# Three edits to the set-up order of a four-layer kernel: transposes of second image halves, the second square root, the next lines

## The chip, the cores and the metric

The kernel runs on one core of a Trainium2 chip. The metric is device time in microseconds of one execution; the figure used is the median of several. A core has five engines with a queue each, worked off in order: TensorE (PE; its weight loads are shown as PEld), VectorE (DVE), ScalarE (ACT), GpSimd (POOL) and SyncE (SP), which here issues most of the DMAs. TensorE writes to banks of PSUM; a bank can be written again only when an engine has copied it out. The operands of all other work lie in SBUF, 128 partitions wide.

## The reference, cut to what matters

The input is 1024 images of 16 x 16 pixels with 16 channels. Four layers follow each other, each of the form x + f(group norm of x):

```python
def _gn(v, G=8, eps=1e-5):
    B_, H_, W_, C_ = v.shape
    g = v.reshape(B_, H_, W_, G, C_ // G)
    m = jnp.mean(g, axis=(1, 2, 4), keepdims=True)
    s = jnp.var(g, axis=(1, 2, 4), keepdims=True)
    return ((g - m) / jnp.sqrt(s + eps)).reshape(v.shape)
...
x = x + _L0_conv_ref(_gn(x), core0, core1, core2)     # tensor train, 4096 x 4096
x = x + _L1_conv_ref(_gn(x), ...)                     # cellular automaton step
x = x + _L2_conv_ref(_gn(x), filters, bias)           # 3 x 3 convolution
x = x + _L3_conv_ref(_gn(x), ...)                     # cellular automaton step
```

Only the start of the first layer matters here. There an image is a vector of 16 x 16 x 16 values, and the layer multiplies it by a 4096 x 4096 matrix given by three small cores. Ahead of that the images have to be normalised: per image and per group of two channels, minus the mean, times one over the root of the variance.

## The kernel before, in words

**Order.** Every engine works off its instructions in exactly the order in which the program emits them (manual schedule); waits between engines are put in where data or a buffer demands them. So the place of a call in the program is its place in the queue of each engine that it uses, SP's DMA queue among them. `now(steps)` emits steps at once. `run(main, us, loads, *spans)` emits the steps of a phase one after the other, and weaves background steps in between: a span `(steps, lo, hi)` spreads its steps, by their weights, from the fraction `lo` to the fraction `hi` of the phase's main steps.

**Layer 0.** The 1024 images are worked in two chunks of 512; chunk 0 is the first to be set up. The matrix product is done by a Strassen-like scheme: 13 phases (`NP`, list `OUTER`), each with four units of seven products (`INNER`), each product two main steps of four matmuls of a 128 x 256 block, in the profile `po` L1693. Phase 0 has 56 main steps. Its order is made by hand: steps 0 to 7 are the products 0 and 2 of units 0 and 1, then follow the rest of unit 0 (steps 8 to 17), of unit 1 (18 to 27), and units 2 and 3. The weights of a unit's products are built on TensorE from 32 small matmuls into four banks (`build`, L1579), copied out by ScalarE (L1584) and combined by VectorE (`mix`, L1608 and L1610). The products are gathered from their banks by ScalarE (L1737) and VectorE (L1731, L1741), and at the end of a unit `store` writes them to memory (L1666).

**Set-up of chunk 0** (`first_images`). The images of chunk 0 arrive as eight pieces of 1024 KB: `load(half, bg)`, with four groups of 128 images (`bg`) and two halves of the 16 image rows. Groups 0 and 1 (i = 0) are fetched first, groups 2 and 3 (i = 1) later; the pieces lie in the tile of pair 1 (`XN[1]`) until that pair's lines come in.
- `stats` and `aggregate` (VectorE, L1116 and L1149) make mean and variance per image and group.
- `turn` fills one bank with four 128 x 128 transposes on TensorE (L1123), and ScalarE copies the bank out. For the first half of the rows the copy goes into a raw block of tile 0 (L1126), `raw_block(wh, i)`; for the second half it goes into a line tile (L1130), and every second bank the line tile is stored to the scratch tensor `xr` in memory by SP (`kept`, L1136, 512 KB). `turns(half, i, wh)` is four such banks. The banks rotate over two tags, one with a single buffer, one with four.
- `keep(wh, i)` stores a whole raw block to `xr` too (L1136, 1024 KB).
- `root(i)` adds epsilon on VectorE (L1153) and takes the square root on ScalarE (L1154); `newton(i)` refines the reciprocal on VectorE (L1158 to L1162); `widen(k, i)` spreads mean (k = 0) or reciprocal root (k = 1) over the row (L1169); `spread(k, i)` turns that with two transposes (L1177) and a copy on ScalarE (L1178).
- `first_normed(b, i)`, called x00, x10, x01 and x11, takes the mean away and scales, two steps each on VectorE (L1280). Block x11 is written over its own raw block; the sums of blocks (`combined`, L1309) are written over the others.

**Around it.** `early` builds a part of the core's weights and, after the second group of loads, stores them to `g_dram` (`keep_g`, L652 and L659, twelve DMAs on SP). `rest` is twelve further pieces of these weights, woven into phase 0 at fixed steps: TensorE (L645), a copy on ScalarE to one small buffer (L697), and after every second piece again six stores on SP (L652, L659); the next piece's copy has to wait for them, since the buffer is the same. `gload` fetches weights for a coming unit (L1546, 256 KB). `part_steps(1)` prepares the lines of pair 1 for phase 1: three loads of 1024 KB from `xr` by SP (L1338), a pause, eight steps of centring and scaling, the fourth load, eight more (all L1280), saves to memory (L1344), then additions (L1348, L1421, L1431): 32 steps of equal weight on VectorE in all.

The dictionary `before` at L2214 says which pieces of set-up are emitted ahead of which main step of phase 0.

Of the kernel before, what the change touches and what calls it, by code (L numbers as in the profile page):

```python
# [105 lines left out]
def conv_preact_kernel(ctx: ExitStack, tc: tile.TileContext, a: dict, out: bass.AP):  # L106
# [1175 lines left out]
    def first_normed(b, i):  # L1282

        X, E = part_tile(0)
        cols = slice(256 * i, 256 * i + 256)

        def op(t, k):
            x = X[:, b, t : t + 4, i]
            centre_scale(x, raw_block(b, i)[:, t : t + 4], 0, cols, k)

        return [(1.2, lambda t=t, k=k: op(t, k)) for t in (0, 4) for k in range(2)]
# [826 lines left out]
    def run(layer, us, loads, *spans, by=0.0):  # L2118

        start, main = layer
        start()
        loads, done = list(loads), 0
        todo = []
        for bg, lo, hi in spans:
            bg = [b if isinstance(b, tuple) else (1, b) if callable(b) else (b, None) for b in bg]
            idle = sum(b[0] for b in bg if b[1] is None) / (us * (hi - lo))
            less = min(1.0, 0.7 / idle) if idle else 1.0  # L2130
            weight = sum(b[0] for b in bg if b[1] is not None) or 1.0
            at = lo
            for cost, step in bg:
                if step is None:
                    at += cost * less / us
                else:
                    todo.append((at, step))
                    at += (hi - lo) * (1 - idle * less) * cost / weight
        todo.sort(key=lambda x: x[0])
        for i, step in enumerate(main):  # L2140
            step()
            part = (i + 1) / len(main)
            while done < len(loads) and done < len(loads) * part / (by or 1e-9):
                loads[done]()
                done += 1
            while todo and (todo[0][0] < part or i == len(main) - 1):
                near = getattr(step, "dense", True) or i == len(main) - 1
                if getattr(todo[0][1], "beside", False) and not near:
                    break
                todo.pop(0)[1]()  # L2150
# [7 lines left out]
    def steps_of(*more):  # L2158
        return (lambda: None), [x for m in more for x in m]

    def now(steps):
        for step in steps:
            step = step[1] if isinstance(step, tuple) else step
            if callable(step):
                step()
# [5 lines left out]
    with ExitStack() as es:  # L2171
# [3 lines left out]
        load, stats, turns, keep, aggregate, root, newton, widen, spread = first_images(tag)  # L2175
        for bg in range(2):
# [12 lines left out]
        stats(1, 1)  # L2189
        aggregate(0)  # L2190
        aggregate(1)
        now(turns(0, 0, 0))
        root(0)
        widen(0, 0)
        newton(0)
# [8 lines left out]
        x00, x11, x10, x01 = (first_normed(*at) for at in ((0, 0), (1, 1), (1, 0), (0, 1)))  # L2204
# [3 lines left out]
        now(x10[0::2] + x10[1::2])  # L2208
        mix(1, "s2")
        now(more[0:2])  # L2210
        half1 = [turns(1, i, 0) + turns(1, i, 1) for i in range(2)]
        late0, late1 = turns(0, 1, 0), turns(0, 1, 1)
        rest = rest[0] + rest[1]
        before = {  # L2214
# [2 lines left out]
            + late1[:2],  # L2217
            5: [lambda: keep(1, 0), lambda: keep(0, 0)],
            6: late1[2:] + [lambda: keep(1, 1)] + late0[:2],
            8: late0[2:] + [lambda: build(1, 0), lambda: keep(0, 1)] + half1[0][:4]  # L2220
            + [lambda: root(1), lambda: widen(0, 1), lambda: newton(1)]
            + half1[0][4:] + [lambda: spread(0, 1), lambda: widen(1, 1)]
            + half1[1][:2] + [lambda: spread(1, 1)]
            + x11[0::2] + x11[1::2] + half1[1][2:4],
            9: [catch_up] + more[2:6],
            10: rest[:1],
            11: rest[1:2] + x01[0::2] + x01[1::2],
# [13 lines left out]
        def sums_late(j):  # L2241
            c = combined(j)
            woven_into(j, {2 * k + 1: c[2 * k : 2 * k + 2] for k in range(5)})
# [2 lines left out]
        woven_into(0, before)  # L2246
        for j in late:
            sums_late(j)
        run(steps_of(phases[0]), 107, (), (part_steps(1), 0.3, 0.99))
        loads, stat, lines, tail, more = input_steps(["m", "w"], G)  # L2250
        tail += [(0, more[0]), 2, (0, more[1]), 2]
        stat = [[stat[0][i] for i in range(4)], [(2.6, s1[1]) for s1 in stat[1][0::2]], stat[1][1::2]]
# [8 lines left out]
        root = {}  # L2261
# [89 lines left out]
```

## Time and profile before

| | us |
|---|---|
| median of 3 runs | 2723.96 (2723.88 to 2724.68) |
| the profiled execution, its own time | 2722.89 |
| its span, from the first to the last instruction | 2720.6 |
| TensorE, 0 to 10 us | busy 3.60 |
| 10 to 20 us | busy 6.37 |
| 20 to 30 us | busy 7.43 |
| 50 to 60 us | busy 7.90 |
| 60 to 70 us | busy 8.11 |
| 100 to 130 us | busy 30.00 |

How to read the lines that follow further down. A line of the timeline gives the start of a group of like instructions, how long the group took, the engine (PE, PEld, DVE, ACT, POOL; SPq is SyncE issuing DMAs), the line of the program, the operation, what it writes and reads, how many there were, and in brackets how long the engine had been idle before it and what released it. A line of the table by stretches gives a stretch in us from the start, its length, the busy time of PE, PEld, DVE, ACT and POOL with the number of instructions, the granted clock of TensorE as a share of full speed, the busy share of the DMA engines, and GB/s moved.

### The profile page before, as it was taken

The page shows a single profiled execution, that of the slowest core. Times are in us where ns is not written, and L with a number is a line of the kernel's source. Part 1 is how long each engine was busy: PE and PEld are TensorE (multiplying, and loading weights), DVE is VectorE, ACT ScalarE, POOL GpSimd, SP SyncE. Part 2 cuts the span into 40 slices and gives each one's busy share as a digit, 9 for nine tenths or more (in the row PEclk, how much of TensorE's full clock was granted, in tenths as well). Part 3 has the DMA queues.
Part 4 walks back from the last instruction along what each step waited for, and adds up shares of the span by engine and source line. Part 5 has one row for each costly group of instructions (what it writes and reads, how often), then busy time and mean ns, then how long its engine had stood idle before and what let it go on. Part 6 is the DMA issues. An engine that isn't in the chain of part 4 may idle for free.

```text
span 2720.6 us, 47297 instructions
## 1 busy us (share of the span) xinstructions
PE 2662.2 (98%) x18990; PEld 1744.2 (64%) x18990; DVE 1994.4 (73%) x2422; ACT 1241.3 (46%) x2094; POOL 539.2 (20%) x701
## 2 busy tenths in 40 slices
PE   7999999999999999999999999999999999999997
PEld 6888888888888888888778633333333333334344
DVE  8796768867787777577878677658778858856654
ACT  5224222222232222333322376776767757666664
POOL 1011352221132633212322111111113211110000
PEclk9999999999999999999999999999999999999998
DMA  8787788988796887887679764455576865444665
GB/s 284 240 314 244 223 190 226 241 180 222 193 237 181 171 197 198 201 237 232 198 170 265 155 158 101 107 163 120 108 188 93 200 161 134 96 89 119 180 173 210
DMA packets 273450, 503.20 MB, mean 185 GB/s; under 512 B 34868, under 2 KB 113256, under 8 KB 263952
## 3 DMA queue, kind: packets, MB, share of 16 engines
q1 hardware_dynamic: 188528, 342.97, 37.9%
q0 software_dynamic: 84512, 157.08, 33.6%
q8 instruction: 150, 2.46, 0.4%
q14 instruction: 68, 0.56, 0.1%
q10 hardware_dynamic: 192, 0.13, 0.0%
HBM read 280.66 MB, written 226.49 MB: 186 GB/s over the span
## 4 chain that ended last, share of the span: by engine, by line
PE 87%; DVE 7%; DMA 2%; issue 1%; ACT 1%; SPq 1%; POOL 0%; DVEq 0%; ACTq 0%
PE po L1693 43%; PE ph L2105 21%; PE po L1934 8%; PE po L1789 5%; PE pw L1579 4%; PE po L1798 1%; DMA xn<-xf 1%; PE ptx L1998 1%; DVE xn L1280 1%; DVE xn L1309 1%; PE ptin L1215 1%; DVE u L1946 0%; DVE s L1608 0%; DMA xn<-in_L_conv_fc_w_dram 0%; DVE xn L778 0%
## 5 line engine op out<-in xcount | busy, mean ns | idle before, releaser
L2108 ACT ACTIVATE hid<-ph,pack 128x512 f32<-128x512 f32 (+1 forms) x1040 | 641.7, 684 | 311.7 <-PE ph L2105 252.6
L1693 PE MATMUL po<-xn,s 128*128 128x256 f32 x3328 | 748.8, 381 | 7.2 <-DVE s L1608 5.1
L1693 PEld LDWEIGHTS po<-xn,s 128*128 128x128 f32 x3328 | 624.7, 190 | 108.8 <-issue 10.8
L1693 PE MATMUL po<-xn,w 128*128 128x256 f32 x2480 | 562.7, 382 | 2.5 <-DVE xn L1309 1.8
L2105 PE MATMUL ph<-xn,wq 32*128 32x512 f32 (+1 forms) x3752 | 518.1, 590 | 1.9 <-DVE u L1946 1.5
L1693 PEld LDWEIGHTS po<-xn,w 128*128 128x128 f32 x2480 | 466.6, 190 | 75.9 <-issue 5.9
L1584 ACT COPY w<-pw 128x512 f32<-128x512 f32 x412 | 211.5, 599 | 443.1 <-PE pw L1579 370.7
L2105 PEld LDWEIGHTS ph<-xn,wq 32*128 32x128 f32 x3752 | 233.9, 184 | 228.5 <-issue 209.8
L2105 PE MATMUL ph<-xn,pack 32*128 32x512 f32 x1288 | 273.8, 607 | 4.5 <-DVE u L1946 1.6
L1608 DVE TENSOR_TENSOR s<-w 128x1024 f32<-128x1024 f32 x205 | 247.7, 1218 | 16.8 <-PE po L1693 15.9
L1934 PE MATMUL po<-hid,pack 128*32 128x512 f32 (+1 forms) x2080 | 256.0, 592 | 0.8 <-ACT hid L2108 0.5
L1946 DVE SCALAR_TENSOR_TENSOR u<-po,pack,xn 128x512 f32<-128x512 f32 (+1 forms) x130 | 96.3, 741 | 168.2 <-PE po L1934 167.1
L1988 POOL DMA_DIRECT2D xf<-u x96 | 82.6, 860 | 617.5 <-DVE u L1986 591.0
L778 DVE TENSOR_TENSOR xn<-xn,m 128x1024 f32<-128x1024 f32 x128 | 150.2, 1217 | 34.6 <-ACT m L801 34.5
L2105 PEld LDWEIGHTS ph<-xn,pack 32*128 32x128 f32 x1288 | 115.0, 184 | 89.6 <-issue 63.4
L1934 PEld LDWEIGHTS po<-hid,pack 128*32 128x32 f32 x2080 | 53.9, 109 | 174.9 <-ACT hid L2108 86.3
L1789 PE MATMUL po<-xn,convw 128*128 128x512 f32 x368 | 163.6, 598 | 0.0
L1309 DVE TENSOR_TENSOR xn<-xn 128x1024 f32<-128x1024 f32 x130 | 152.6, 1215 | 0.0
L1731 DVE TENSOR_TENSOR r<-r,po 128x1024 f32<-128x1024 f32 x77 | 93.8, 1218 | 72.1 <-PE po L1693 64.1
L1664 POOL DMA_DIRECT2D xf<-xn x69 | 90.2, 1771 | 250.9 <-DVE xn L1657 70.5
L1579 PE MATMUL pw<-R,gq 32*128 32x128 f32 x3264 | 134.9, 284 | 0.0
L1579 PEld LDWEIGHTS pw<-R,gq 32*128 32x128 f32 x3264 | 109.9, 187 | 33.8 <-issue 31.5
(249 smaller groups left out, 2777.0 us busy)
## 6 DMA issues: line engine op xcount, KB each, us to landing
xn<-xf SPq DMA_DIRECT2D x128, 512.0 KB
xn<-xb SPq DMA_DIRECT2D x36, 1024.0 KB
wq<-L_conv_wy SPq DMA_DIRECT2D x192, 192.0 KB
xf<-xn POOLq DMA_DIRECT2D x69, 512.0 KB, 9.9
piece<-xb SPq DMA_DIRECT2D x64, 512.0 KB
xf<-r POOLq DMA_DIRECT2D x48, 512.0 KB, 12.0
xf<-u POOLq DMA_DIRECT2D x96, 256.0 KB, 4.0
gq<-g_dram SPq DMA_DIRECT2D x84, 256.0 KB
```

Of the source, the lines that this page charges most:

```text
L778: V.tensor_tensor(part, part, m().unsqueeze(1).broadcast_to([P, 2, NB]), op)
L1309: V.tensor_tensor(out, y, z, f)
L1579: T.matmul(pw[r][:, v, i], g[rows, P * (2 * v + i) : P * (2 * v + i) + P], R[rows, k], start=k == 0, stop=k == len(gs) - 1,)
L1584: A.copy(w.rearrange("p b s t m -> p (b s t) m")[:, :, 32 * r : 32 * r + 32].rearrange("p k (v o) -> p v k o", v=2), pw[r].rearrange("p v ...
L1608: V.tensor_tensor(t.rearrange("p s t m -> p (s t m)"), x, y, f)
L1693: T.matmul(po[:, i], matrix(u, what)[:, i, t], x, start=t == 0, stop=t == 3)
L1731: V.tensor_tensor(part, part, po.unsqueeze(2).broadcast_to([P, 2, 2, 256]), ALU.add)
L1789: T.matmul(st["po", h][wh], conv["fw"][:, y], X[:, 16 * wh + h + y - 1], start=y == max(0, 1 - h), stop=y == min(2, S - h),)
L1934: T.matmul(po[32 * j : 32 * j + 32], nca["w1"][:, v], hid[j], start=v == 0, stop=v == 1)
L1946: V.scalar_tensor_tensor(u, po, nca["b1"], X[:, 8 * q + w2, cols(hf)], ALU.add, ALU.add)
L2105: T.matmul(ph, w, x, start=k == 0, stop=k == len(tiles) - 1)
L2108: A.activation(h, ph, AF.Relu, bias=nca["bt"][:, r : r + 1])
```

## The change

Three things move; nothing is added or left out.
1. Six of the eight banks of `half1[0]` (the second half of the rows for image groups 0 and 1) are transposed right behind the first four banks, ahead of `root(0)`. The line tiles of these banks are stored to `xr` from there, three DMAs on SP.
2. Ahead of step 8, `root(1)`, `widen(0, 1)` and `newton(1)` come before the remaining two banks of `half1[0]` and before `build(1, 0)`, which goes behind `spread(1, 1)`; fewer banks stand ahead of the two `spread` calls, and three banks of `half1[1]` instead of two stand behind them, ahead of x11.
3. `part_steps(1)` is spread over 0.26 to 0.95 of phase 0 instead of 0.3 to 0.99.

```diff
-        now(turns(0, 0, 0))
+        half1 = [turns(1, i, 0) + turns(1, i, 1) for i in range(2)]
+        now(turns(0, 0, 0) + half1[0][:6])
         root(0)
         widen(0, 0)
         newton(0)
...
         now(more[0:2])
-        half1 = [turns(1, i, 0) + turns(1, i, 1) for i in range(2)]
         late0, late1 = turns(0, 1, 0), turns(0, 1, 1)
...
-            8: late0[2:] + [lambda: build(1, 0), lambda: keep(0, 1)] + half1[0][:4]
-            + [lambda: root(1), lambda: widen(0, 1), lambda: newton(1)]
-            + half1[0][4:] + [lambda: spread(0, 1), lambda: widen(1, 1)]
-            + half1[1][:2] + [lambda: spread(1, 1)]
-            + x11[0::2] + x11[1::2] + half1[1][2:4],
+            8: late0[2:] + [lambda: keep(0, 1), lambda: root(1), lambda: widen(0, 1)]
+            + [lambda: newton(1)] + half1[0][6:] + [lambda: spread(0, 1), lambda: widen(1, 1)]
+            + half1[1][:1] + [lambda: spread(1, 1), lambda: build(1, 0)] + half1[1][1:4]
+            + x11[0::2] + x11[1::2],
...
-        run(steps_of(phases[0]), 107, (), (part_steps(1), 0.3, 0.99))
+        run(steps_of(phases[0]), 107, (), (part_steps(1), 0.26, 0.95))
```

## The prediction

> **What bounds the kernel now.** I read the page's span, engine and chain lines first, then the order of instructions from 0 to 215 us, the waits of TensorE in that stretch, and the DMA traffic stage by stage.
>
> ```profile
> span 2720.6 us, 47297 instructions
> PE 2662.2 (98%) x18990; PEld 1744.2 (64%) x18990; DVE 1994.4 (73%) x2422; ACT 1241.3 (46%) x2094; POOL 539.2 (20%) x701
> PE 87%; DVE 7%; DMA 2%; issue 1%; ACT 1%; SPq 1%; POOL 0%; DVEq 0%; ACTq 0%
> ```
>
> TensorE is busy 98% of the span, so only its idle time, and time in which it runs slowly, can be had back: 2720.6 - 2662.2 = 58.4 us at most, and most of that lies ahead of 160 us, where the change is. Later work is TensorE's own, so what is gained or lost at 160 us should stay to the end. The rows of this stretch, first the set-up:
>
> ```profile
> 17.83 0.59 ACT L1126 COPY xn<-ptin 128x512 f32<-128x512 f32 x1 [0.27 <-PE ptin L1123]
> ...
> 22.01 0.21 ACT L1154 ACTIVATE small<-small 128x16 f32<-128x16 f32 x1 [3.59 <-DVE small L1153]
> ...
> 22.57 1.91 PE L1123 MATMUL ptin<-ident,xn 128*128 128x128 f32 x8
> ...
> 39.55 1.04 PE L1123 MATMUL ptin<-ident,xn 128*128 128x128 f32 x8
> ```
>
> ScalarE waits 3.59 us for the first root: this is the hole that the change fills. Eight transposes take 1.91 us at 22.57, after TensorE had been idle for 4.30 us, and 1.04 us at 39.55, the same work.
>
> ```profile
> 59.66 4.63 DVE L1280 TENSOR_TENSOR xn<-xn 128x1024 f32<-128x1024 f32 x4 [1.34 <-ACT xn L1178]
> ...
> 63.21 3.72 PE L1693 MATMUL po<-xn,s 128*128 128x256 f32 x16 [1.82 <-DVE xn L1280]
> ...
> 81.02 5.41 PE L1693 MATMUL po<-xn,w 128*128 128x256 f32 x16 [1.78 <-DVE xn L1309]
> ```
>
> Block x11 is normalised by VectorE from 59.66 us; TensorE waits for it until 63.21. VectorE then has no gap until TensorE waits for it again at 81.02, and there 16 matmuls take 5.41 us where they take 3.72 elsewhere (granted clock 0.64 over 80 to 84 us).
>
> **The first part: six banks in the wait.** The copies of the first four banks start at 15.19 to 17.83, 0.88 us apart; the later pairs start 1.37 us apart (54.24 and 55.61), 0.69 a bank. Six more end at 18.42 + 6 x 0.69 = 22.6 to 18.42 + 6 x 0.88 = 23.7, and the first square root stands behind them on ScalarE: 0.6 to 1.7 us later than 22.01. Behind it come VectorE's refinement and the first block. But VectorE waited 0.75 us at 29.03 for ScalarE's weight copies anyway, so -0.1 to +1.0 reaches the chain of VectorE that runs from 30 to 51 us. I take +0.3. It is covered, as the next part shows, by a wait at 58 us; without that cover it would cost itself.
>
> **The second part: second root sooner.** In the kernel before, VectorE ends the aggregation at 50.98 us, but the root waits on ScalarE until 56.57 behind weight copies and two halves. Moved up it starts near 51.3. From the root's start to the end of the widening took 56.57 to 58.32, 1.75 us, so x11 could start near 53.1 instead of 59.66: 6.5 us. TensorE's own rest there (two and four banks of transposes at 0.52 us, two small transposes, 1.17 us of weight building, ScalarE's 2.05 us of copies between) ends near 57. Two small costs lie under the same cover: an odd number of banks ahead of spread(1, 1) puts it on the bank of the transposes just before, 0.6 us for their copy, and build(1, 0) comes 2 us later, whose weights are first read after step 9.
>
> But x11 is written over its raw block, and that block's store to memory (keep, the third of four) must have read it. SP's queue is in order, and here the moved banks issue something: three stores of 512 KB, which follow the g_dram writes and stand **ahead** of the four keeps:
>
> ```profile
> 42.36 9.27 SPq L1136 DMA_DIRECT2D xr<-xn  x4
> ...
> 44.00:54.00 10.00, 9.08 (x81) 7.50 (x79) 7.42 (x35) 4.90 (x10) 0.00 (x0) 1.00 1.04 346
> 54.00:58.00 4.00, 2.60 (x20) 2.13 (x21) 0.99 (x6) 3.60 (x8) 0.00 (x0) 1.00 0.91 303
> ```
>
> The last two columns are the DMA share and GB/s: the DMA is full. From 26 to 42 us it moved 16 x 369 GB/s = 5.90 MB, to 44 us another 0.51: the second half of the images (four of 1024 KB) and the g_dram writes, together 6.29 MB, were through by 43.6, with 0.13 MB of the keeps (1024 KB each). Before, the third keep thus ended (3.15 - 0.13) / 0.346 = 8.7 us past 44, at 52.7, and nobody felt it. Now 1.57 MB go first: (4.72 - 0.13) / 0.346 = 13.3, at 57.3. With an estimated 0.7 us to the release (the first image's bytes were in by 8.7 by the traffic, and its statistics began at 9.26), x11 starts at **58.0**, 1.6 us sooner than before, not 6.5. Bounds: at 369 GB/s 57.1 (2.5 sooner), at 303 59.8 (0.2 later). VectorE's order behind x11 is unchanged and has no gap, so 81.02 becomes 79.4.
>
> **The clock.** TensorE now has nothing from about 57 until the first half of x11 is scaled at 61.5. The stretch from 79.24 to 81.02, 1.78 us idle, was followed by 1.69 us of loss (5.41 - 3.72). If the same comes at 61.5, TensorE arrives at 79.4 without the 1.78 us of slack it had, so that costs nothing, and the loss at 81 goes away: the shift is 1.6 without and 3.3 with this.
>
> [...]
>
> **The third part: pair 1 lines sooner.** part_steps(1) has 32 steps of weight and 8 us of pause over 0.69 of the 56 steps of phase 0, both before and after; all moves by 0.04 x 56 = 2.2 steps. The three loads (0.30 x 56: after step 16; now 0.26 x 56: after step 14) are 1024 KB each and pass the six g_dram writes of step 16 on SP:
>
> ```profile
> 88.35 1.24 SPq L652 DMA_DIRECT2D g_dram<-xn  x2
> 89.64 2.95 SPq L659 DMA_DIRECT2D g_dram<-xn  x4
> 92.69 1.60 SPq L1338 DMA_DIRECT2D xn<-xr  x3
> ...
> 94.71 0.77 ACT L697 COPY xn<-pg 128x128 f32<-128x128 f32 x4 [6.39 <-DMA g_dram<-xn]
> 95.73 0.98 PEld L1579 LDWEIGHTS pw<-R,gq 32*128 32x128 f32 x32 [0.33 <-ACT xn L697]
> ```
>
> ScalarE's copy of the next piece waits for these writes, and TensorE's weight building waits for the banks that this copy frees; before, it came just in time (TensorE was busy to 95.8). Now: the last line stores go out near 79.7 (81.3 before) and end near 81.4; three loads at 380 to 396 GB/s (the rate of 96 to 100 us, with such loads in it) take 8.1, to 89.5; the 256 KB of weights behind them 0.7, to 90.2; the writes, 1.05 MB at 260 GB/s (their rate from 92 to 94), 4.0, to 94.2, and some 0.5 to the release: **94.7**, as before. So whatever TensorE won, 1.6 or 3.3 us, ends in a wait for ScalarE at 95.7. Bounds: loads at 426 GB/s (the image loads at 30 to 34 us) 0.7 sooner; at 303 2.3 later. I take 0.
>
> The fourth load is a gain. It stood after step 29, behind that step's g_dram writes and result stores:
>
> ```profile
> 136.37 1.23 DVE L1280 TENSOR_TENSOR xn<-xn,xn 128x1024 f32<-128x1024 f32 x1 [7.54 <-DMA xn<-xr]
> ...
> 138.79 3.72 PE L1693 MATMUL po<-xn,w 128*128 128x256 f32 x16 [0.73 <-DVE w L1610]
> ...
> 147.92 1.99 PE L1693 MATMUL po<-xn,s 128*128 128x256 f32 x8 [0.73 <-DVE s L1608]
> ```
>
> Eight steps of 0.0192 past 0.375 is 0.529 of the phase, step 29; now 0.489, step 27. SP is free from 109.4 to 118.3, and the DMA is at 0.44 from 110 to 120, so it lands long before its use. VectorE's 7.54 us stall goes, and with it TensorE's two waits: 0.73 + 0.73 = **1.46**. What is late next I don't see: TensorE waits 0.7 us at a time for ScalarE from 197 on, as before.
>
> **The sum.** 0 at 95.7, and -1.46: the profiled execution took 2722.89 (span 2720.6), which becomes 2721.4; the median of the runs, 2723.96, is 1.07 above it, so **2722.5**. Its own range is 2721.8 to 2724.2: the wait 0.7 sooner, or the idle before it followed by one stretch of half clock, 1.69.
>
> **Rivals.** (a) The wait at 95 does not bind, because the loads run beside the writes: then the shift at 81 passes, 1.6 + 1.46 = 3.1 or 3.3 + 1.46 = 4.8: 2720.9 to 2719.2. For it: 94.7 holds only if the queue is served strictly in order. Against: that is what the byte counts at 43.6 and 52.7 need.
> (b) x11 does not wait for its keep: TensorE resumes near 57.8, 5.4 sooner, with 1.46 and perhaps 1.69: 2717.1 to 2715.4, if the wait at 95 falls too. Against: the block is scaled in place.
> (c) Slower: the g_dram writes land late behind the three loads. Place: ScalarE's copy at 94.71. From 1.46 us later on the change loses; at 303 GB/s it is 2.3, and the idle before it, 1.78 us and more, brings 1.69 of half clock: 2.3 + 1.69 - 1.46 = +2.5, 2726.5; with the writes at 174 GB/s (the mean of 88 to 94) two more, 2728.5, and a second slow stretch takes it past 2729.4.
> (d) The early hole is no hole: the root 1.7 us later, uncovered: 2724.
>
> **How the numbers follow.** Forecast 0.42 (with d), (a) 0.18, (b) 0.13, (c) 0.27. About 0.2%, 5.4 us, is what a measurement of this kernel can tell from no change: faster is (b) and a little of (a), 0.16; slower the far end of (c), 0.14; 0.70 between. The range, 2717.5 to 2727.5, leaves out most of (b) and the end of (c).
>
> **What would show it.** Three line stores ahead of the keeps on SP; x11 released by a DMA near 58 us; TensorE idle before it, half clock after it and none at 81; the loads ahead of the g_dram writes and TensorE waiting for ScalarE near 95; no 7.5 us stall of VectorE near 130. I am wrong if x11 starts near 53, or if TensorE passes 95 us without a wait.

## The result, and the profile after

The changed kernel is slower: median 2730.86 us (2729.26 to 2734.86, 12 runs) against 2724.70 us for the kernel before (2722.34 to 2729.21, 12 runs), a ratio of 1.0023 with a 95% interval of 1.0016 to 1.0031. That is above the forecast range, which ended at 2727.5. Its profiled execution took 2731.45 us, with a span of 2729.5.

The timeline of the changed kernel, the lines that answer to those shown of before. First the set-up and block x11:

```profile
23.36 0.23 ACT L1154 ACTIVATE small<-small 128x16 f32<-128x16 f32 x1
...
29.57 1.22 DVE L1608 TENSOR_TENSOR s<-w 128x1024 f32<-128x1024 f32 x1
...
43.47 2.43 SPq L1136 DMA_DIRECT2D xr<-lines  x3
...
46.00 8.27 SPq L1136 DMA_DIRECT2D xr<-xn  x4
...
51.75 0.22 ACT L1154 ACTIVATE small<-small 128x16 f32<-128x16 f32 x1
...
61.02 4.63 DVE L1280 TENSOR_TENSOR xn<-xn 128x1024 f32<-128x1024 f32 x4 [7.53 <-DMA xr<-xn]
...
64.56 5.49 PE L1693 MATMUL po<-xn,s 128*128 128x256 f32 x16 [6.79 <-DVE xn L1280]
...
82.37 3.72 PE L1693 MATMUL po<-xn,w 128*128 128x256 f32 x16
```

The first root is 1.35 us later (23.36 against 22.01), the second 4.82 sooner (51.75 against 56.57). But VectorE then waits 7.53 us for a DMA, the store of the raw block, and x11 starts 1.36 us **later** than before. TensorE idles 6.79 us and then does 16 matmuls in 5.49 us (granted clock 0.50 from 64.5 to 68 us). At 82.37, where it had waited for VectorE and been slow, it does neither: 3.72 us (granted clock 1.00 from 82 to 85 us) against 5.41 in the kernel before (0.50 from 82 to 84 us). One profile of each kernel does not settle differences of 1 to 2 us here: with the new set-up x11 starts at 59.58 (e1) and 59.96 us (e9) as well, and with the old one at 61.86 (e5), though nothing ahead of it differs.

Then the loads of pair 1's lines and the piece of the weights behind them:

```profile
83.94 2.12 SPq L1338 DMA_DIRECT2D xn<-xr  x3
...
88.01 1.25 SPq L652 DMA_DIRECT2D g_dram<-xn  x2
89.31 4.07 SPq L659 DMA_DIRECT2D g_dram<-xn  x4
...
95.39 0.49 PE L1579 MATMUL pw<-R,gq 32*128 32x128 f32 x4
...
99.49 0.77 ACT L697 COPY xn<-pg 128x128 f32<-128x128 f32 x4 [11.51 <-DMA g_dram<-xn]
...
100.15 2.24 PE L1579 MATMUL pw<-R,gq 32*128 32x128 f32 x28 [4.26 <-ACT xn L697]
...
102.31 5.39 PE L1693 MATMUL po<-xn,s 128*128 128x256 f32 x16
```

The loads now go out ahead of the six g_dram writes. ScalarE's next copy waits 11.51 us for these writes and starts at 99.49 instead of 94.71; TensorE gets four of its 32 small matmuls done, waits 4.26 us for the banks, and is slow after it (granted clock 0.50 from 99 to 105 us). In the kernel before, the group of matmuls that now starts at 102.31 came right behind the building:

```profile
96.83 3.72 PE L1693 MATMUL po<-xn,s 128*128 128x256 f32 x16
```

Last, the end of phase 0 in the changed kernel:

```profile
121.67 0.43 SPq L1338 DMA_DIRECT2D xn<-xr  x1
...
145.14 3.72 PE L1693 MATMUL po<-xn,w 128*128 128x256 f32 x16
```

The fourth load is there in time; VectorE's stall of 7.54 us and TensorE's two waits of 0.73 us are gone. The same instruction of TensorE in both profiles, side by side:

| TensorE's instruction | before | after | difference |
|---|---|---|---|
| first matmul on x11 | 63.21 | 64.56 | +1.35 |
| next wait for VectorE | 81.02 | 82.37 | +1.35 |
| the group after it | 87.39 | 87.06 | -0.33 |
| weight building | 95.73 | 95.39 | -0.34 |
| the group after it | 96.83 | 102.31 | +5.48 |
| the next piece | 100.48 | 107.64 | +7.16 |
| group that waited for `w` (L1610) | 138.79 | 145.14 | +6.35 |
| a late group of phase 0 | 156.17 | 161.53 | +5.36 |
| first transposes of chunk 1 (L1215) | 191.1 | 196.5 | +5.4 |

The loss is made in one place, between 95 and 108 us: from the building to the group behind it 6.92 us instead of 1.10, 4.26 of it the wait and 1.56 slow work, and that group 5.33 instead of 3.65, 1.68 more of slow work: 7.5 in all. The fourth load gives 1.8 back. The two spans differ by 8.9 us, 3.5 more than the profiles do at 196 us; the medians differ by 6.2. Of these 3.5 us 3.2 arise between the first transposes of chunk 1 and TensorE's first matmul on the hidden values of the second layer (L1934): 1357.6 us in the changed kernel and 1354.4 in the one before. The ten profiles other than that of before take 1356.5 to 1358.2 there, e2 and e5 with the old set-up among them, so the profile of before is the odd one, and no cause is claimed.

### The profile page after: what moved, and what is told of

Its sections match the earlier page's. It is cut to its first block, busy times and chain, and to the rows that moved or that the text cites. A ratio compares the mean times of both kernels' runs of the same rounds, so it can differ in the third digit from the quotient of the medians.

```text
span 2729.5 us, 47301 instructions
## 1 busy us (share of the span) xinstructions
PE 2664.3 (98%) x18990; PEld 1745.1 (64%) x18990; DVE 1994.6 (73%) x2422; ACT 1241.1 (45%) x2094; POOL 538.0 (20%) x701
## 4 chain that ended last, share of the span: by engine, by line
PE 86%; DVE 7%; DMA 4%; issue 1%; ACT 1%; SPq 0%; POOL 0%; DVEq 0%; ACTq 0%; POOLq 0%
PE po L1693 42%; PE ph L2105 21%; PE po L1934 8%; PE po L1789 5%; PE pw L1579 4%; PE po L1798 1%; DMA xn<-xr 1%; DMA m<-means 1%; DMA xn<-xf 1%; PE ptx L1998 1%; DVE xn L1280 1%; DVE u L1946 1%; PE ptin L1215 1%; DVE s L1608 1%; PE pg L645 0%
## 5 line engine op out<-in xcount | busy, mean ns | idle before, releaser
L1934 PE MATMUL po<-hid,pack 128*32 128x512 f32 (+1 forms) x2080 | 256.0, 592 | 0.8 <-ACT hid L2108 0.5
L1934 PEld LDWEIGHTS po<-hid,pack 128*32 128x32 f32 x2080 | 53.9, 109 | 174.9 <-ACT hid L2108 86.3
L1579 PEld LDWEIGHTS pw<-R,gq 32*128 32x128 f32 x3264 | 110.4, 187 | 38.3 <-issue 32.2
```

What stands on the lines that cost most here:

```text
L1579: T.matmul(pw[r][:, v, i], g[rows, P * (2 * v + i) : P * (2 * v + i) + P], R[rows, k], start=k == 0, stop=k == len(gs) - 1,)
L1934: T.matmul(po[32 * j : 32 * j + 32], nca["w1"][:, v], hid[j], start=v == 0, stop=v == 1)
```

## The experiments

The theory after these traces: **the order on SP's queue** costs, at two places. The three loads pass the g_dram writes and bring the wait near 96; the three line stores pass the keeps and eat what the sooner root had won. The rival: the set-up edits cost by themselves, and the sooner lines gain.

| kernel | median us | ratio to before, 95% | first transposes of chunk 1 in its profile |
|---|---|---|---|
| before | 2724.63 and 2725.05 | | 191.1 |
| changed | 2730.86 | 1.0023 (1.0016 to 1.0031) | 196.5 |
| e1, lines back | 2724.66 | 1.0002 (0.9993 to 1.0011) | 190.0 |
| e2, sooner lines alone | 2731.80 | 1.0023 (1.0014 to 1.0031) | 198.0 |
| e3, stores behind | 2727.58 | 1.0011 (1.0002 to 1.0020) | 191.6 |
| e4, stores behind, lines back | 2721.98 | 0.9991 (0.9982 to 1.0000) | 188.6 |
| e5, fourth load alone | 2723.35 | 0.9994 (0.9985 to 1.0003) | 189.9 |
| e6, e4 with the fourth load | 2722.14 | 0.9990 (0.9981 to 0.9999) | 185.1 |
| e7, piece first | 2725.36 | 1.0000 (0.9992 to 1.0009) | 189.6 |
| e8, stores behind, piece first | 2722.82 | 0.9990 (0.9981 to 0.9999) | 187.7 |
| e9, filler | 2732.57 | 1.0032 (1.0020 to 1.0044) | 195.5 |

e1 to e4 shared 33 runs of the kernel before, e5 to e8 another 33; e9 had 10 (median 2724.09).

**e1: the changed kernel without the sooner lines.**

```diff
-        run(steps_of(phases[0]), 107, (), (part_steps(1), 0.26, 0.95))
+        run(steps_of(phases[0]), 107, (), (part_steps(1), 0.3, 0.99))
```

> The changed kernel with part_steps(1) spread over 0.3 to 0.99 again; the two set-up edits stay. Theory (the loss sits at the pair 1 loads, which pass the g_dram writes of step 16): ScalarE's copy after step 18 no longer waits 11.5 us, TensorE no longer waits 4.3 us near 96 and the half clock after it is gone, but VectorE's stall on the fourth load and TensorE's two waits of 0.73 us are back; about as the kernel before, 2722 to 2726. Rival (the set-up edits cost by themselves, x11 at 61.0 instead of 59.7 and the half clock after it): 2728 or more.

2724.66 us, a ratio of 1.0002: no difference from before. The whole loss hangs on this one line. Its timeline:

```profile
59.58 4.63 DVE L1280 TENSOR_TENSOR xn<-xn 128x1024 f32<-128x1024 f32 x4 [7.48 <-DMA xr<-xn]
...
63.13 6.36 PE L1693 MATMUL po<-xn,s 128*128 128x256 f32 x16 [6.74 <-DVE xn L1280]
...
81.65 3.62 PE L1693 MATMUL po<-xn,w 128*128 128x256 f32 x16
...
93.60 0.77 ACT L697 COPY xn<-pg 128x128 f32<-128x128 f32 x4 [6.44 <-DMA g_dram<-xn]
...
137.68 3.72 PE L1693 MATMUL po<-xn,w 128*128 128x256 f32 x16 [0.78 <-DVE w L1610]
```

The wait for the keep (7.48 us) and the slow matmuls after it (6.36) are here too and cost nothing: at 81.65 TensorE no longer waits. So the set-up edits alone make no difference that 11 runs can show (the interval spans some 2.5 us to either side), and the rival, 2728 or more, falls.

**e2: the kernel before with the sooner lines alone** (the same line, the other way round).

> The kernel before with part_steps(1) over 0.26 to 0.95, nothing else. Theory: the three loads, issued near 82 us, push the g_dram writes back, ScalarE's copy starts near 97 to 99 instead of 94.7, TensorE waits 2 to 4 us near 96 and then runs at half clock for a stretch; the waits at 138 and 148 go (1.5 us); in sum 2 to 6 us slower than before, 2726 to 2730. Rival (set-up edits cost by themselves, sooner lines gain): 1 to 2 us faster than before.

2731.80 us, as slow as the whole change, and more than was expected. The timeline:

```profile
85.05 2.15 SPq L1338 DMA_DIRECT2D xn<-xr  x3
...
100.63 0.77 ACT L697 COPY xn<-pg 128x128 f32<-128x128 f32 x4 [12.11 <-DMA g_dram<-xn]
```

ScalarE's copy starts 15.6 us after the first of the loads is issued, as in the changed kernel (83.94 to 99.49).

**e3 and e4: the line stores behind the third keep**, with the sooner lines (e3) and without (e4).

```diff
             if h % 4:
-                kept(wh, i, 6 + h, st["l"])
+                go = lambda x=st["l"]: kept(wh, i, 6 + h, x)
+                held_back.append(go) if holding[0] else go()
...
-            6: late1[2:] + [lambda: keep(1, 1)] + late0[:2],
+            6: late1[2:] + [lambda: keep(1, 1), release] + late0[:2],
```

`release` sends the three stores held back and ends the holding.

> The changed kernel, but the line stores of the six early banks are issued only behind the third keep on SP. Theory (x11 waits for the keep, and the keep for 1.5 MB of line stores): x11 starts near 53.5 instead of 61.0 and TensorE resumes near 58 instead of 64.6 without a long idle stretch; the loads then go out near 77, and the wait for ScalarE near 95 remains in part; 3 to 6 us faster than the changed kernel, 2724 to 2728. Rival (x11's wait is for something else than this order): x11 within 1 us of 61 and a time within 1.5 us of the changed kernel's.

> Both: line stores behind the third keep, and part_steps(1) over 0.3 to 0.99. Theory: x11 near 53.5, TensorE resumes near 58, 5 us sooner than in the kernel before, nothing waits for ScalarE near 95; the two waits of 0.73 us remain; 4 to 7 us faster than before, 2717 to 2720. Rival (what is won at x11 is taken by VectorE, which then bounds, or by the DMA): no more than 2 us faster than before.

e3 takes 2727.58, 3.3 us less than the changed kernel; e4 takes 2721.98, 2.7 less than e1 and than before. The long wait of VectorE for the keep is gone in both, which the first theory needs; the rival of an x11 that does not move is out. The gain of e4 is smaller than the 4 to 7 us expected. Its timeline shows why:

```profile
54.05 2.36 DVE L1287 TENSOR_TENSOR xn<-xn 128x1024 f32<-128x1024 f32 x2 [0.72 <-DMA xr<-xn]
...
55.66 0.59 ACT L1136 COPY lines<-ptin 128x512 f32<-128x512 f32 x1 [2.44 <-DMA xr<-lines]
...
56.30 0.44 PE L1184 MATMUL ptmr<-ident,wide 128*128 128x128 f32 x2 [3.13 <-ACT lines L1136]
...
61.11 3.18 PE L1700 MATMUL po<-xn,s 128*128 128x256 f32 x13
...
78.14 5.41 PE L1700 MATMUL po<-xn,w 128*128 128x256 f32 x16 [0.89 <-DVE xn L1316]
```

x11 starts at 54.05, 5.5 us sooner than in e1. But the stores held back hold their line tiles: ScalarE waits 2.44 us for one of the four to come free, TensorE's second small transposes wait for ScalarE, and the last banks of the halves stand behind them. TensorE is at x11 at 61.11, 2.1 us sooner than before. A wait for one DMA became a wait for another. Slower work takes a part too: the 12 transposes at 58.49 take 2.82 us, where they take 1.53 in the changed kernel, and at 78.14 16 matmuls take 5.41, as in the kernel before, where e1 loses nothing (3.62 at 81.65).

The waits of TensorE from 30 to 170 us in e3 (what waited, for what, us in total, times, longest):

```profile
PE pw L1586 <- ACT xn L697: 3.7, 1, 3.7
PE ptmr L1184 <- ACT lines L1136: 2.5, 1, 2.5
```

The first line is the wait near 96 again (the line numbers of these kernels are higher by 6 and 7). With TensorE at x11 at 62.00, 2.6 us sooner than in the changed kernel, the loads go out at 79.89 and ScalarE's copy starts at 95.55, 15.7 us later. TensorE begins the building at 92.06, 3.7 us sooner than in the kernel before (95.73), and the wait of 3.7 takes just that.

**e5 and e6: the fourth load alone**, on the kernel before and on e4. It is moved from behind the eighth to behind the fourth of the first eight steps.

```diff
-            if p == 1 and j == 1:
-                steps.append(loads[3])
...
                         steps.append((0, lambda p=p, wh=wh: save(first[p], wh, 0, 4, lines(p, wh))))
+                        if j == 1 and (p, wh) == (0, 0):
+                            steps.append(loads[3])
```

> The kernel before, with only the fourth load of pair 1's lines moved, from behind the eighth to behind the fourth of the first eight steps, with its span at 0.3 to 0.99. Theory (what the sooner lines gain is this load alone): VectorE's stall of 7.5 us and TensorE's two waits of 0.7 us near 138 and 148 go, ScalarE's copy near 94.7 stays where it was; 1 to 2 us faster than before. Rival (the load pushes other DMAs back): the same as before or slower, with a new wait of TensorE between 100 and 130 us.

> The two set-up edits with the line stores behind the third keep, the span at 0.3 to 0.99, and the fourth load behind the fourth step. Theory (the gains add): TensorE 2.8 us sooner at 100 us as in the run with the stores behind and the lines back, and 1.5 us more past 150; 3.5 to 5.5 us faster than before, 2719 to 2721. Rival (they do not add, since VectorE bounds): 2.5 to 3 us faster than before, as without the fourth load.

e5 is 1.7 us faster by the medians, the size expected, but its interval (0.9985 to 1.0003) holds no change. In its profile the two waits and VectorE's stall are gone. e6 has TensorE 6.0 us sooner at the first transposes of chunk 1, and the table by stretches shows no idle time from 110 to 160 us (columns: length, busy time and number of TensorE's matmuls, granted clock, DMA share, GB/s):

```profile
110.00:160.00 50.00, 50.00 (x362) 1.00 0.79 260
```

Yet it is 2.9 us faster in time (0.9990, 0.9981 to 0.9999), below what was expected, as much as the rival forecast, and no faster than e4. The rival's reason, VectorE as the bound, does not show up to 160 us, and where the other 3 us go is not settled: TensorE's first matmul on the hidden values of the second layer comes at 1542.0, 3.5 sooner than the 1545.5 of before. The profile of before is quicker than every other from the first transposes of chunk 1 to there (1354.4 us against 1356.9 in e6), so the 2.5 us between may not be lost by e6 at all.

**e7 and e8: the other order, with the sooner lines kept.** The piece of step 16 goes to the end of step 14, so its six writes stand ahead of the loads on SP again; e8 has the line stores behind the third keep besides.

```diff
-            14: rest[2:3] + half1[1][6:],
-            16: rest[3:4],
+            14: rest[2:3] + half1[1][6:] + rest[3:4],
```

> The changed kernel, with the weights' piece of step 16 moved to the end of step 14, so that its six g_dram writes stand ahead of the three loads on SP again; span 0.26 to 0.95 and the line stores unchanged. Theory (it is the order on SP, not the earlier lines): ScalarE's 11.5 us wait and TensorE's 4.3 us wait near 96 go; 5 to 8 us faster than the changed kernel, 2722 to 2725. Rival (the DMA's load near 90 us is too high in any order): the wait near 96 stays over 2 us and the time above 2727.

> The changed kernel with both orders on SP mended: line stores behind the third keep, and the piece of step 16 at the end of step 14. Theory: x11 near 54 to 56, no wait near 96, no waits near 138 and 148; 3.5 to 6 us faster than before, 2718.5 to 2721. Rival (something else of the change costs): not faster than 2722.

e7 takes 2725.36, a ratio of 1.0000, 5.5 us less than the changed kernel. ScalarE's copy there:

```profile
91.51 0.78 ACT L697 COPY xn<-pg 128x128 f32<-128x128 f32 x4 [7.52 <-PE pg L645]
```

It waits for its own matmuls and for no DMA. SP's queue, in the same profile:

```profile
85.31 3.33 SPq L659 DMA_DIRECT2D g_dram<-xn  x4
88.74 1.63 SPq L1338 DMA_DIRECT2D xn<-xr  x3
```

The lines have the same place in the program as in the changed kernel, and the loads are as large: it is the order. It moves both sides: the first two of the six writes go out at 84.01 instead of 88.01, and the loads at 88.74 instead of 83.94; the run does not tell the two apart. The time, 5.5 us below the changed kernel's, is 0.4 outside the 2722 to 2725 expected. e8 takes 2722.82, faster than before (0.9981 to 0.9999), but by 2.2 us: outside the 2718.5 to 2721 expected and on the side of its rival (not faster than 2722). TensorE's wait for ScalarE and a line tile, 3.1 us in e4, is 4.0 us there; no run shows whether that is all that is missing.

**e9: TensorE kept busy in the wait.** The result of these transposes is never read.

```diff
+                if at == 5 and u == 1:
+                    fill = bank([P, 4, P], "m", "fill")
+                    for _ in range(7):
+                        for l in range(4):
+                            T.transpose(fill[:, l], ident, ident)
                 if at == 5 and u > 0:
                     build(u + 1, 0)
```

> The changed kernel with 28 transposes of the identity, whose result nobody reads, on TensorE ahead of the weight building that waits for ScalarE near 96 us (28 x 0.13 = 3.7 us, inside the wait of 4.3). Theory (part of the loss is TensorE's half clock after that wait): the building takes 1.2 instead of 2.2 us and the 16 matmuls behind it 3.7 instead of 5.4; 1.5 to 3 us faster than the changed kernel, 2727.5 to 2729.5. Rival (the half clock is not set by the idle time, or the wait simply ends later): within 1 us of the changed kernel's 2730.9 or slower.

```profile
94.25 3.22 PE L1704 MATMUL fill<-ident 128*128 128x128 f32 x28
...
100.03 1.36 PE L1579 MATMUL pw<-R,gq 32*128 32x128 f32 x28 [2.15 <-ACT xn L697]
101.32 5.33 PE L1693 MATMUL po<-xn,s 128*128 128x256 f32 x16
```

The expectation fails: the filler takes 3.22 us, 2.15 us of idle time remain, the building runs fast (1.36) and the matmuls behind it still take 5.33 (granted clock 0.65 from 100 to 104 us). The time, 2732.57, is not below that of the changed kernel. So the half clock's share of the loss, 3.2 us by the trace, was not shown by a run of its own; that a shorter wait leaves the larger part of it in place was.

## Why the prediction was wrong

- **What the lines cost.** The step that failed is the landing of the g_dram writes at "94.7, as before", and with it the 0 that I took at 95.7: ScalarE's copy started at 99.49, and TensorE waited 4.26 us, to 100.15. The 94.7 was worked out from a last line store "near 79.7", right ahead of the loads; it went out at 83.45. From that store to the copy I had 15.0 us, the last 0.5, to the release, an estimate that no run shows by itself; it took 16.0 (changed kernel) and 16.1 (e2, e3). So 1.0 of the 4.8 us is the length and 3.8 the start. SP reaches the loads when TensorE and ScalarE have turned the last lines. TensorE began these transposes not 1.6 us sooner than before but 3.13 later (81.28 against 78.15): 1.35 from x11 and 1.77 from the half clock behind it (5.49 against 3.72, at a granted clock of 0.50 against 1.00). That half clock I had forecast and called free, since the wait at 81 pays for it; but these transposes, and the loads behind them, stand ahead of that wait. With the wait gone TensorE also follows the store more closely: it is at the building 11.9 us after it, where it had been 14.4 (81.35 to 95.73), so a copy 16.0 us after it comes too late. The 81.35 itself was one profile's: with the old set-up it is 84.57 in e2 and 84.60 in e5. Rival (c), its place, its queue and the half clock after it, is what happened; its price of +2.5 was too small, since the start was too early and one stretch of half clock of 1.69 stood for the 3.2 measured.
- **x11.** The wait for the keep was right, its end was not: 61.02 us instead of 58.0, outside the bounds of 57.1 to 59.8 (59.58 in e1, 59.96 in e9). By the traffic the 11.0 MB up to the third keep had passed by 58.5, 1.2 us later than counted; the release came 2.5 us after that and not 0.7. The second group of images was fetched 1.5 us later than before (26.31 against 24.81), which is not shown to come from the edits: with the old set-up it was 26.45 in e2. With the stores behind, in e4, x11 starts at 54.05, near the 53.1 worked out for the root.
- **The clock.** Half clock after the long idle time at 61 us, with the wait at 81 gone: right (5.49 and 3.72 in the changed kernel, at a granted clock of 0.50 and 1.00; 6.36 and 3.62 in e1); the loss of 1.69 forecast was 1.77 and, in e1, 2.64. The length of the wait alone does not settle it: waits of 6.79 and 4.26 us in the changed kernel, 1.78 us in the kernel before and 2.15 us in e9 were followed by slow matmuls (5.49, 5.39, 5.41 and 5.33 us for 16), and so was one of 0.89 us at 78.14 in e4 (5.41), but 1.82 us at 63.21 in the kernel before was not (3.72, at a granted clock of 1.00).
- **The first root.** Later by 1.35 us, inside 0.6 to 1.7, but 0.96 of that was there ahead of the moved banks (the fourth copy of the first four banks starts at 18.79 instead of 17.83); at 29.57 instead of 29.03, +0.5 was left of it. In e1, with the same set-up, the root came at 21.97, no later than before.
- **The fourth load.** Right: -1.46 forecast; the row at 138.79 and the next ones give back 1.8 in the changed kernel, and e5 alone is worth 1.7 by its medians, though its interval holds no change.
- **Rival (a)** would have needed the loads beside the writes; e7 against the changed kernel shows that their order decides. **Rival (b)** fell with VectorE's 7.53 us wait for the store.
- **What can be had ahead of 160 us.** Not most of the 58.4 us, as the prediction has it: TensorE is busy 139.9 of the first 160 us, so 20.1 us of its idle time lie there and 38.3 behind. That a gain at 160 us stays to the end does not follow, and of the 6.0 us of e6 at 185 us 3.5 were left at 1542 in the profiles.

## What to carry to other kernels

A step moved forward takes its DMAs along, and these pass others on their queue (here on SP: the loads at 83.94 us, ahead of the writes at 88.01; in e7 the writes at 84.01, ahead of the loads at 88.74); look for whoever waits for the passed ones, here a small buffer that the next piece overwrites (a wait of 11.51 us) and a block that is scaled in place (7.53 us). Three loads of 1 MB, first used 9 us later, cost TensorE 7.5 us in the profile when they were put ahead of six small stores, twice the hole of 3.6 us in the set-up that the change filled. By the trace of e5, only the one late load had to move to end the waits near 138 and 148 us; the 1.7 us that this gains are not clear of noise.

## What the runs showed that was not expected

Filling a wait with idle work did not keep TensorE at full clock: 2.15 us without work, after 3.22 us of filler, were followed by 16 matmuls of 5.33 us (granted clock 0.65 from 100 to 104 us). What sets the granted clock no run shows. And a store's release came 2.5 us after the bytes up to it had passed by the count (2.5 and 2.6 in e1 and e9), where I had estimated 0.7 from a load. With the line stores behind the keeps it came 1.0 to 1.2 us after (e3, e4, e6, e8), with the DMA as busy: a share of 0.84 (e6) and 0.82 (e8) over the first 60 us, 0.82 in the changed kernel. The cause is open.
